# Quartered products of a four-layer graph network: three sums of the close formed in two GpSimd additions and one VectorE addition, and a new order of the products

## The chip, the cores and the metric

The kernel runs on one core of a Trainium2 chip. A core has five engines that run side by side, each taking its instructions in order: TensorE (PE in the profile; its weight loads are PEld) multiplies matrices and writes only to PSUM, an accumulator memory of eight banks; VectorE (DVE) and ScalarE (ACT) work element by element and read PSUM and SBUF, the on-chip working memory; GpSimd (POOL) works element by element in SBUF; SyncE (SP) issues DMA transfers. Semaphores order the engines among each other. The metric is the time on the device in microseconds (us), the median of several runs; lower is better.

## The reference

The input x has 128 graphs of 64 nodes with 512 features, fp32, and one 64x64 adjacency matrix. Four layers follow one another, each with h = relu(layernorm(x)) ahead of it and a residual sum after it:

```
layer 0:  q,k,v = h@Wq+bq, h@Wk+bk, h@Wv+bv  (8 heads of 64)
          x += softmax(q k^T / 8 + mask) v
layer 1:  the same, then @ Wo + bo
layer 2:  rel = adj^T * (q k^T);  rel /= norm(rel, axis=2);  x += rel v     (no heads)
layer 3:  as layer 1 without biases on q,k,v; o = attn @ w_proj + b_proj;  x += o + layernorm(o)*gamma + beta
```

## The kernel before

The rows of x (128 x 64 = 8192) are cut into 16 tiles of 512 rows. The loop over n = 0..63 goes through the layers, and within each layer through the 16 tiles. For a tile, `layer_norm` makes h, turns it with DMA transposes into hT (ScalarE copies hT out of the transposed halves hp), and `sums_x` forms the sums S on GpSimd that the fast matrix products need. Then the projections follow: q, k, v in layers 0, 1 and 3; in layer 2 g = h @ (Wq^T Wk), which has been folded once (`a2`), and v (`v2`). In layers 1 and 3 an output projection o of the tile before follows. Attention (`scores`, `attend`, `values`) or `relate` (layer 2) stands between.

Each projection is a 512x512x512 product, computed by Winograd's form of Strassen's scheme: seven products of 256-wide halves, numbered 1 to 7, in place of eight. On PE one such product is four fp32 matmuls of 128x128 weights and 256 columns, recorded as eight. `projection` runs through them in a written order. Products 1 and 2 add up in one PSUM bank, 6 and 7 in a second, 5 and 3 in a third; product 4 has its own. Between the two of a bank, its content is read out: after 1, `s1` is a copy on ScalarE; after 6, `u2` is a VectorE sum of the bank and s1; after 5, `z5` is a copy on ScalarE; after 7, `u3` is a VectorE sum again. Four quadrants of the output come from them:

- Y11: the bank of 1 and 2, a copy on ScalarE (with the bias in layer 1's q and k)
- Y12: the bank of 5 and 3, plus u2, on VectorE
- Y22: u3 + z5, on GpSimd
- Y21: product 4, plus u3

In layers 1, 2 and 3 (the names in LEVEL2) product 4 is quartered: the same scheme is used once more on 128-wide quarters, seven small products in place of eight. Its part "4a" holds the small products 1, 5, 6, 4, and "4b" the small products 2, 7, 3, added on top of 4a in the same bank. Each part is a group of 128-column matmuls, eight records and six. After 4a, ScalarE copies two quarters of the bank into a small tile q (q0 and z5), and VectorE forms u2 = quarter + q0. 4b may add onto these quarters only when they have been read. After 4b, VectorE forms u3 = quarter + q0, and `close_2` finishes: three GpSimd additions put the shared sums into the base (the big u3, or the output tile in layer 3's o), and two VectorE additions of the bank and the base write Y21. 159 projections are quartered: 16 tiles times q, k, v, o in layer 1, g, v in layer 2, q, k, v, o in layer 3, without the last o. The last tile's v has an order of its own, LAST_V.

The order in which all this is issued is not the order of the code. `Plan` records every step with its readers and writers, and `Plan.order` schedules them in a model of the five queues: of the steps of an engine that are ready it takes the one of lowest rank. The rank is the place in the recorded order, less RUSH = 100 places for a step that reads a PSUM bank (a tile named mm_), and ahead of all for the later steps of scores and values. So PE can take another product in between, or swap two, where the plan holds one as not ready. Pool.take and Pool.give hand the eight banks round, oldest first.

The orders are these tuples; ORDER serves layer 0, and FINER the quartered projections:

```
ORDER = (1, 6, 5, 2, 7, 3, 4)
FINER = (1, 6, 5, "4a", 2, 7, 3, "4b")
LAST_V = (1, 6, "4a", 5, 7, "4b", 2, 3)
```

The profile puts every instruction on one line, L221, since the plan issues them all there; tiles tell them apart. In the profile's names mm is a bank, u the tiles u2 and u3, s the tile s1 (and the attention scores), z the tile z5 (and others), q the small tile of the quartered product, xo the output tile of layer 1's o (it shares its buffers with the residual rows), kT also the output tile of layer 3's o.

Of the kernel before, what the change touches and what calls it, by code (L numbers as in the profile page):

```python
# [14 lines left out]
AF = mybir.ActivationFunctionType  # L15
# [3 lines left out]
P = 128  # L19
G = 64  # L20
D = 512
# [21 lines left out]
BLOCKS = {1: W11, 2: W21, 3: W22, 4: WT4, 5: WT1, 6: WT2, 7: WT3}  # L43
ORDER = (1, 6, 5, 2, 7, 3, 4)

FINER = (1, 6, 5, "4a", 2, 7, 3, "4b")
LAST_V = (1, 6, "4a", 5, 7, "4b", 2, 3)
ORDER0 = (1, 2, 5, 6, 3, 7, 4)

# [9 lines left out]
class Plan:  # L59
# [4 lines left out]
    def __init__(self, nc):  # L64
        self.nc = nc
        self.steps, self.products, self.lags, self.front = [], [], {}, set()
        self.wrote, self.readers, self.known = {}, {}, {}
        self.group = None
        for e in ("tensor", "vector", "scalar", "gpsimd", "sync"):
            setattr(self, e, Engine(self, e))  # L70

# [79 lines left out]
    def order(self):  # L151
        n = len(self.steps)
        wait = [0] * n
        users = [[] for _ in range(n)]
        for i, s in enumerate(self.steps):
            lags = {**self.lags.get(i, {}), **{d: 0.0 for d in s[2]}}
            wait[i] = len(lags)
            for d, lag in lags.items():
                users[d].append((i, lag))

        rank = [i - (n if i in self.front else 0) - RUSH * any(v.tensor.name.startswith("mm_") for c in s[1] for v in c[1][1:] if isinstance(v, bass.AP)) for i, s in enumerate(self.steps)]
        ready = [0.0] * n
        free = {e: 0.0 for e in ("tensor", "vector", "scalar", "gpsimd", "sync")}
        added = 0.0
        moved = 0.0
        port = 0.0
        soon = {e: [] for e in free}
        here = {e: [] for e in free}
        for i in range(n):
            if not wait[i]:  # L170
                heapq.heappush(soon[self.steps[i][0]], (0.0, rank[i], i))
        out = []
        while len(out) < n:
            best = None
            for e in free:
                while soon[e] and soon[e][0][0] <= free[e]:
                    heapq.heappush(here[e], heapq.heappop(soon[e])[1:])
                if here[e]:
                    at = free[e]
                elif soon[e]:  # L180
                    at = soon[e][0][0]
                else:
                    continue
                if best is None or at < best[0]:
                    best = (at, e)
            at, e = best
            if not here[e]:
                while soon[e] and soon[e][0][0] <= at:
                    heapq.heappush(here[e], heapq.heappop(soon[e])[1:])
            i = heapq.heappop(here[e])[1]  # L190
            eng, calls, _, busy, late = self.steps[i]
            moves = calls[0][0] == "dma_start"
            if e == "gpsimd":
                busy += max(0.0, port - at)
            if moves and e == "gpsimd":
                moved = max(moved, at) + 8000
                added = max(added + 6000, at + 8500)
                late = added - at - busy
            elif e == "sync":
                moved = max(moved, at + 1400) + late / (170 if calls[0][2].get("transpose") else 280)  # L200
                late = moved + 600 - at - busy
            elif e == "vector" and late == PORT:
                busy += max(0.0, free["gpsimd"] - at)
                port = at + busy
            free[e] = at + busy
            out.append((at, i))
            for u, lag in users[i]:
                same = self.steps[u][0] == e
                ready[u] = max(ready[u], at + busy - lag + (0.0 if same and not moves else late))
                wait[u] -= 1  # L210
                if not wait[u]:
                    heapq.heappush(soon[self.steps[u][0]], (ready[u], rank[u], u))
        self.start = {i: at for at, i in out}
        self.span = max(free.values())
        return [i for _, i in sorted(out)]
# [90 lines left out]
def gnn_stack_kernel(  # L306
# [293 lines left out]
    def quarter(t, prod, i, j):  # L600
        u, v = (j, i) if prod is prod_T else (i, j)
        return t[:, u, v * P : (v + 1) * P]
# [8 lines left out]
            a, b = (ws[i], x) if prod is prod_T else (x, ws[i])  # L611
            pe.matmul(out, a, b, start=i == 1, stop=True, skip_group_check=True)

    def close_2(prod, ps, q, base, dst, bias):

        u2, u3, z5 = q[:, 1], q[:, 2], q[:, 3]
        y12 = quarter(base, prod, 0, 1)
        gps.tensor_tensor(y12, y12, u2, ALU.add)
        y2 = base[:, :, P:] if prod is prod_T else base[:, 1, :].rearrange("p (v f) -> p v f", v=2)
        gps.tensor_tensor(y2, y2, u3.unsqueeze(1).to_broadcast([P, 2, P]), ALU.add)  # L620
        gps.tensor_tensor(dst[:, 1, P:], base[:, 1, P:], z5, ALU.add)
        for at in ((slice(None), 0, slice(None)), (slice(None), 1, slice(0, P))):
            if bias is None:
                dve.tensor_tensor(dst[at], ps[at], base[at], ALU.add)
            else:
                dve.scalar_tensor_tensor(dst[at], ps[at], bias[at[1]], base[at], ALU.add, ALU.add)

    def projection(prod, name, xop, nm, emit, order=None):
        w = W[name]
        order = order or (FINER if finer(name) else ORDER)  # L630

        banks = {}
        tmp = {}

        def bank(i):
            banks[i] = mm.take(f"{i}_{nm}")
            return banks[i]

        def tmp_tile(tag):
            tmp[tag] = p1.tile([P, D], F32, tag=tag, name=f"{tag}_{nm}")  # L640
            return tmp[tag]

        X = {1: 1, 2: 1, 6: 6, 7: 6, 5: 5, 3: 5, 4: 4, "4a": "4a", "4b": "4a"}
        for i in order:
            home = X[i]
            first = home == i
            ps = bank(home) if first else banks[home]
            plan.begin()
            if i in BLOCKS:
                prod(ps, w[:, BLOCKS[i]], xop()[i], first)  # L650
            else:
                pv = ps.rearrange("p (u v) -> p u v", u=2)
                prod_2(prod, pv, name, xop(), (1, 5, 6, 4) if i == "4a" else (2, 7, 3))
            plan.end()
            if i == 1:
                act.copy(tmp_tile("s1"), ps)
            elif i == 2:
                emit("Y11", ps)
            elif i == 6:
                dve.tensor_tensor(tmp_tile("u2"), ps, tmp["s1"], ALU.add)  # L660
                emit("u2", tmp["u2"])
            elif i == 5:
                emit("z5", ps, tmp_tile("z5"))
            elif i == 7:
                dve.tensor_tensor(tmp_tile("u3"), ps, tmp["s1"], ALU.add)
                emit("u3", tmp["u3"])
                emit("Y22", tmp["u3"], tmp["z5"])
            elif i == 4:
                emit("Y21", ps, tmp["u3"])
            elif i == 3:  # L670
                emit("Y12", ps, tmp["u2"])
            elif i == "4a":
                q = p1.tile([P, 4, P], F32, tag="q", name=f"q_{nm}")
                act.copy(q[:, 0], quarter(pv, prod, 0, 0))
                dst, base, bias = emit("close")
                if bias is None:
                    act.copy(q[:, 3], quarter(pv, prod, 0, 1))
                else:
                    act.activation(q[:, 3], quarter(pv, prod, 0, 1), AF.Identity, bias=bias[1])
                dve.tensor_tensor(q[:, 1], quarter(pv, prod, 1, 1), q[:, 0], ALU.add)  # L680
            elif i == "4b":
                dve.tensor_tensor(q[:, 2], quarter(pv, prod, 1, 1), q[:, 0], ALU.add)
                if base is None:
                    base = tmp["u3"].rearrange("p (u v) -> p u v", u=2)
                close_2(prod, pv, q, base, dst, bias)
            if i in (2, 7, 3, 4, "4b"):
                mm.give(f"{home}_{nm}")
            if i != order[-1]:
                yield
# [3 lines left out]
    def emit_plain(region, shared=gps):  # L693

        def emit(what, a=None, b=None):
            if what == "close":
                return region(1, 0), None, None
            if what in ("u2", "u3"):
                return
            if what == "z5":  # L700
# [12 lines left out]
    def emit_bias(region, bias):  # L713

        def emit(what, a=None, b=None):
            if what == "close":
                return region(1, 0), None, (bias[:, 0:1], bias[:, 1:2])
            if what in ("u2", "u3"):
                return
            if what == "z5":  # L720
# [240 lines left out]
    def emit_out3(n, o):  # L961
# [5 lines left out]

        def emit(what, a=None, b=None):
            if what == "close":
                return reg(1, 0), reg(1, 0), None  # L970
            v2 = lambda t: t.rearrange("p (u v) -> p u v", u=2)
            if what == "u2":
                gps.tensor_tensor(v2(a), v2(a), bc(1), ALU.add)
# [332 lines left out]
```

## Time and profile before

| | us |
|---|---|
| median of 3 runs | 2827.89 (2827.47 to 2830.86) |
| profiled execution | 2826.41 |
| its span, first to last instruction | 2824.6 |
| PE busy | 2804.5 (99%) |
| VectorE busy | 1796.5 (64%) |
| ScalarE busy | 1500.7 (53%) |
| GpSimd busy | 1974.4 (70%) |
| granted PE clock | 0.999 |

The busy time of an engine is the time in which it has at least one instruction at work. The chain of work that ended last is on PE for 90% of the span. A row such as "PE mm <- DVE u: 2.2, 1, 2.2" in the list of waits says that PE stood still for 2.2 us in all, once, and that the instruction which let it go was VectorE's that writes u. In rows by form, the numbers after the bar are the busy time in us and the mean of one in ns.

### The profile page before, as it was taken

How to read it: one execution, taken by the hardware profiler on the slowest of the kernel's cores; microseconds unless marked ns; L12 is line 12 of the kernel's file. 1: busy time of each engine (PE TensorE's matmuls, PEld its weight loads, DVE VectorE, ACT ScalarE, POOL GpSimd, SP SyncE). 2: the span in 40 equal slices, each digit the busy share in tenths (PEclk: the TensorE clock that was granted, in tenths of full speed). 3: DMA queues.
4: the chain of work that ended last, by engine and by line, in shares of the span. 5: the costliest groups of instructions: out<-in, count | busy, mean ns of one | idle time of the engine just before them, and what ended most of it. 6: DMA issues, size and time to landing. Idle time of an engine off the chain costs nothing.

```text
span 2824.6 us, 65745 instructions
## 1 busy us (share of the span) xinstructions
PE 2804.5 (99%) x26787; PEld 2482.6 (88%) x26787; DVE 1796.5 (64%) x3346; ACT 1500.7 (53%) x2111; POOL 1974.4 (70%) x2008
## 2 busy tenths in 40 slices
PE   9999999999999999999999999999999999999998
PEld 8888788888888888888888888888888888888887
DVE  6666566765656556556545565655568777677676
ACT  4566557556564654645644444443545546556452
POOL 6555565557867677677678755556788887887885
PEclk9999999999999999999999999999999999999999
DMA  6566567556555555646556766566644655554553
GB/s 157 137 153 149 125 157 149 122 136 157 113 106 109 105 102 105 111 85 109 117 109 122 174 150 161 143 157 154 131 91 91 117 97 91 117 102 91 109 90 64
DMA packets 634447, 343.55 MB, mean 122 GB/s; under 512 B 484257, under 2 KB 565409, under 8 KB 634145
## 3 DMA queue, kind: packets, MB, share of 16 engines
q1 hardware_dynamic: 600880, 273.30, 43.0%
q0 software_dynamic: 33264, 66.06, 14.5%
q8 instruction: 209, 3.42, 0.5%
q14 instruction: 94, 0.76, 0.1%
HBM read 120.10 MB, written 102.76 MB: 79 GB/s over the span
## 4 chain that ended last, share of the span: by engine, by line
PE 90%; POOL 3%; DMA 2%; DVE 2%; ACT 1%; issue 1%; SPq 1%; POOLq 0%; DVEq 0%; ACTq 0%
PE mm L221 90%; POOL S L221 1%; POOL w L221 1%; SPq L221 1%; DMA xin<-in_x_dram 1%; DMA hp<-z 1%; POOL s L221 0%; DVE st L221 0%; ACT s L221 0%; DMA xin<-x 0%; DMA x<-xo 0%; ACT z L221 0%; POOL u L221 0%; DVE u L221 0%; ACT hT L221 0%
## 5 line engine op out<-in xcount | busy, mean ns | idle before, releaser
L221 PE MATMUL mm<-S,w 128*128 128x256 f32 x3584 | 814.5, 380 | 2.2 <-DVE u L221 2.2
L221 PEld LDWEIGHTS mm<-S,w 128*128 128x128 f32 x3584 | 678.5, 190 | 95.3 <-DVE u L221 2.6
L221 PE MATMUL mm<-hT,w 128*128 128x256 f32 (+1 forms) x3040 | 609.0, 346 | 0.0
L221 PEld LDWEIGHTS mm<-hT,w 128*128 128x128 f32 x3040 | 506.8, 191 | 55.4 <-issue 0.5
L221 DVE TENSOR_TENSOR u<-mm,s 128x512 f32<-128x512 f32 x414 | 284.6, 687 | 366.3 <-PE mm L221 295.0
L221 PE MATMUL mm<-w,S 128*128 128x256 f32 x2048 | 470.6, 381 | 1.3 <-ACT z L221 1.2
L221 PEld LDWEIGHTS mm<-w,S 128*128 128x128 f32 x2048 | 385.2, 190 | 55.7 <-ACT z L221 1.6
L221 ACT COPY hT<-hp 128x1024 uint16<-128x1024 uint16 x252 | 333.4, 1352 | 140.0 <-DMA hp<-z 139.5
L221 PE MATMUL mm<-w,hT 128*128 128x256 f32 (+1 forms) x1696 | 349.0, 348 | 2.5 <-DVE s L221 2.5
L221 PEld LDWEIGHTS mm<-w,hT 128*128 128x128 f32 x1696 | 284.4, 191 | 35.0 <-DVE s L221 3.7
L221 POOL TENSOR_TENSOR qT<-u,z 128x512 f32<-128x512 f32 x64 | 86.3, 1348 | 308.7 <-DVE u L221 254.4
L221 ACT COPY s<-mm 128x512 f32<-128x512 f32 x211 | 123.0, 585 | 323.8 <-PE mm L221 242.0
L221 DVE COPY z<-xin 128x1024 uint16<-128x1024 uint16 x252 | 271.9, 1095 | 34.8 <-ACT xin L221 27.2
L221 ACT COPY s<-hp 128x1024 uint16<-128x1024 uint16 x188 | 243.6, 1350 | 8.0 <-DMA hp<-z 7.7
L221 ACT ACTIVATE xin<-xin,nb,rs 128x512 f32<-128x512 f32 x256 | 194.7, 813 | 68.7 <-DVE nb L221 68.6
L221 POOL TENSOR_TENSOR S<-hT 128x512 f32<-128x512 f32 x126 | 162.8, 1292 | 91.6 <-ACT hT L221 91.6
L221 ACT COPY z<-s 128x1024 uint16<-128x1024 uint16 x188 | 192.2, 1047 | 64.8 <-POOL s L221 64.7
L221 PE MATMUL mm<-w,SO 128*128 128x256 f32 x992 | 224.7, 379 | 0.5 <-issue 0.5
L221 POOL TENSOR_TENSOR s<-s,mx 128x1024 f32<-128x1024 f32 x96 | 181.2, 1905 | 58.3 <-DVE mx L221 55.5
L221 POOL TENSOR_TENSOR u<-u,q 128x128 f32<-128x128 f32 (+1 forms) x288 | 180.3, 633 | 54.9 <-DVE q L221 45.4
L221 ACT ACTIVATE s<-s 128x1024 f32<-128x1024 f32 (+1 forms) x112 | 108.0, 967 | 207.8 <-POOL s L221 113.2
L221 PEld LDWEIGHTS mm<-w,SO 128*128 128x128 f32 x992 | 188.0, 190 | 26.1 <-DVE mx L221 0.7
(130 smaller groups left out, 4157.3 us busy)
## 6 DMA issues: line engine op xcount, KB each, us to landing
xin<-x SPq DMA_DIRECT2D x128, 256.0 KB, 3.7
xin<-in_x_dram SPq DMA_DIRECT2D x64, 256.0 KB, 3.8
x<-row POOLq DMA_DIRECT2D x16, 1024.0 KB, 14.0
x<-xo POOLq DMA_DIRECT2D x16, 1024.0 KB, 9.8
xin<-out_dram SPq DMA_DIRECT2D x64, 256.0 KB, 3.6
out_dram<-row POOLq DMA_DIRECT2D x16, 1024.0 KB, 11.1
out_dram<-xo POOLq DMA_DIRECT2D x15, 1024.0 KB, 9.9
out_dram<-xo SPq DMA_DIRECT2D x36, 256.0 KB, 2.5
```

The lines of the kernel that those rows point to most:

```text
L221: getattr(getattr(self.nc, eng), op)(*a, **k)
```

## The change

FINER is reordered: after 4a comes product 7, then 4b, then 3, and product 2 last. VectorE gets one more addition after 4b: z5 += u3 (both 128 x 128 in SBUF). The slots of the tile q are chosen by `shared_2` so that u2 and u3 lie side by side in the order in which their target quarters lie in the base. `close_2` then has two GpSimd additions in place of three: one of 128 x 256 that adds both to the two middle quarters (`mid`), and one of 128 x 128 that writes the last quarter as base + z5. Both are put into `hot`, a set of steps that get the same RUSH in rank as steps that read a bank. The emit functions return `mid` as well. ORDER, LAST_V and layer 0 stay.

```diff
--- before.py
+++ after.py
@@ -43,7 +43,7 @@
 BLOCKS = {1: W11, 2: W21, 3: W22, 4: WT4, 5: WT1, 6: WT2, 7: WT3}
 ORDER = (1, 6, 5, 2, 7, 3, 4)
 
-FINER = (1, 6, 5, "4a", 2, 7, 3, "4b")
+FINER = (1, 6, 5, "4a", 7, "4b", 3, 2)
 LAST_V = (1, 6, "4a", 5, 7, "4b", 2, 3)
 ORDER0 = (1, 2, 5, 6, 3, 7, 4)
 
@@ -66,6 +66,7 @@
         self.steps, self.products, self.lags, self.front = [], [], {}, set()
         self.wrote, self.readers, self.known = {}, {}, {}
         self.group = None
+        self.hot = set()
         for e in ("tensor", "vector", "scalar", "gpsimd", "sync"):
             setattr(self, e, Engine(self, e))
 
@@ -158,7 +159,14 @@
             for d, lag in lags.items():
                 users[d].append((i, lag))
 
-        rank = [i - (n if i in self.front else 0) - RUSH * any(v.tensor.name.startswith("mm_") for c in s[1] for v in c[1][1:] if isinstance(v, bass.AP)) for i, s in enumerate(self.steps)]
+
+        rank = [
+            i - (n if i in self.front else 0)
+            - RUSH * (i in self.hot or any(
+                v.tensor.name.startswith("mm_") for c in s[1] for v in c[1][1:] if isinstance(v, bass.AP)
+            ))
+            for i, s in enumerate(self.steps)
+        ]
         ready = [0.0] * n
         free = {e: 0.0 for e in ("tensor", "vector", "scalar", "gpsimd", "sync")}
         added = 0.0
@@ -611,14 +619,17 @@
             a, b = (ws[i], x) if prod is prod_T else (x, ws[i])
             pe.matmul(out, a, b, start=i == 1, stop=True, skip_group_check=True)
 
-    def close_2(prod, ps, q, base, dst, bias):
-
-        u2, u3, z5 = q[:, 1], q[:, 2], q[:, 3]
-        y12 = quarter(base, prod, 0, 1)
-        gps.tensor_tensor(y12, y12, u2, ALU.add)
-        y2 = base[:, :, P:] if prod is prod_T else base[:, 1, :].rearrange("p (v f) -> p v f", v=2)
-        gps.tensor_tensor(y2, y2, u3.unsqueeze(1).to_broadcast([P, 2, P]), ALU.add)
-        gps.tensor_tensor(dst[:, 1, P:], base[:, 1, P:], z5, ALU.add)
+    def shared_2(prod, q):
+
+
+        i, j = (1, 2) if prod is prod_N else (2, 1)
+        return q[:, 0], q[:, i], q[:, j], q[:, 3]
+
+    def close_2(prod, ps, q, base, mid, dst, bias):
+
+        for a, b, c in ((mid, mid, q[:, 1:3]), (dst[:, 1, P:], base[:, 1, P:], q[:, 3])):
+            plan.hot.add(len(plan.steps))
+            gps.tensor_tensor(a, b, c, ALU.add)
         for at in ((slice(None), 0, slice(None)), (slice(None), 1, slice(0, P))):
             if bias is None:
                 dve.tensor_tensor(dst[at], ps[at], base[at], ALU.add)
@@ -629,8 +640,7 @@
         w = W[name]
         order = order or (FINER if finer(name) else ORDER)
 
-        banks = {}
-        tmp = {}
+        banks, tmp = {}, {}
 
         def bank(i):
             banks[i] = mm.take(f"{i}_{nm}")
@@ -671,18 +681,22 @@
                 emit("Y12", ps, tmp["u2"])
             elif i == "4a":
                 q = p1.tile([P, 4, P], F32, tag="q", name=f"q_{nm}")
-                act.copy(q[:, 0], quarter(pv, prod, 0, 0))
-                dst, base, bias = emit("close")
+                q0, u2, u3, z5 = shared_2(prod, q)
+                act.copy(q0, quarter(pv, prod, 0, 0))
+                dst, base, mid, bias = emit("close")
                 if bias is None:
-                    act.copy(q[:, 3], quarter(pv, prod, 0, 1))
+                    act.copy(z5, quarter(pv, prod, 0, 1))
                 else:
-                    act.activation(q[:, 3], quarter(pv, prod, 0, 1), AF.Identity, bias=bias[1])
-                dve.tensor_tensor(q[:, 1], quarter(pv, prod, 1, 1), q[:, 0], ALU.add)
+                    act.activation(z5, quarter(pv, prod, 0, 1), AF.Identity, bias=bias[1])
+                dve.tensor_tensor(u2, quarter(pv, prod, 1, 1), q0, ALU.add)
             elif i == "4b":
-                dve.tensor_tensor(q[:, 2], quarter(pv, prod, 1, 1), q[:, 0], ALU.add)
+                dve.tensor_tensor(u3, quarter(pv, prod, 1, 1), q0, ALU.add)
+                dve.tensor_tensor(z5, z5, u3, ALU.add)
                 if base is None:
-                    base = tmp["u3"].rearrange("p (u v) -> p u v", u=2)
-                close_2(prod, pv, q, base, dst, bias)
+                    t = tmp["u3"]
+                    base = t.rearrange("p (u v) -> p u v", u=2)
+                    mid = t[:, P : 3 * P].rearrange("p (u v) -> p u v", u=2)
+                close_2(prod, pv, q, base, mid, dst, bias)
             if i in (2, 7, 3, 4, "4b"):
                 mm.give(f"{home}_{nm}")
             if i != order[-1]:
@@ -694,7 +708,7 @@
 
         def emit(what, a=None, b=None):
             if what == "close":
-                return region(1, 0), None, None
+                return region(1, 0), None, None, None
             if what in ("u2", "u3"):
                 return
             if what == "z5":
@@ -714,7 +728,7 @@
 
         def emit(what, a=None, b=None):
             if what == "close":
-                return region(1, 0), None, (bias[:, 0:1], bias[:, 1:2])
+                return region(1, 0), None, None, (bias[:, 0:1], bias[:, 1:2])
             if what in ("u2", "u3"):
                 return
             if what == "z5":
@@ -967,7 +981,8 @@
 
         def emit(what, a=None, b=None):
             if what == "close":
-                return reg(1, 0), reg(1, 0), None
+                mid = o.rearrange("p t d -> p (t d)")[:, 2 * D + P :][:, : 2 * (D - P)]
+                return reg(1, 0), reg(1, 0), mid.rearrange("p (u v) -> p u v", u=2)[:, :, :P], None
             v2 = lambda t: t.rearrange("p (u v) -> p u v", u=2)
             if what == "u2":
                 gps.tensor_tensor(v2(a), v2(a), bc(1), ALU.add)
```

## The prediction

> **What bounds the kernel now.** I read the page's busy line first.
>
> ```profile
> PE 2804.5 (99%) x26787; PEld 2482.6 (88%) x26787; DVE 1796.5 (64%) x3346; ACT 1500.7 (53%) x2111; POOL 1974.4 (70%) x2008
> ```
>
> TensorE (PE) is busy for all but 20 us of the 2824.6 us span. The list of waits, for PE alone, says what is left to gain.
>
> ```profile
> PE mm L221 <- ACT xin L221: 2.5, 1, 2.5
> PE mm L221 <- DVE s L221: 2.5, 2, 1.7
> PE mm L221 <- DVE u L221: 2.2, 1, 2.2
> PE mm L221 <- POOL ident masks.py:199: 1.4, 1, 1.4
> PE mm L221 <- ACT z L221: 1.2, 1, 1.2
> PE mm L221 <- DVE kT L221: 1.2, 3, 0.6
> ...
> ```
>
> Columns: total us, times, longest. With three small rows (0.5, 0.4, 0.2) PE waits 12.1 us in all. 3.9 of these (xin, ident) belong to the start of the program. Busy time by stretches, cut at the layer boundaries, shows where the other 8.2 are not.
>
> ```profile
> 650.00:1477.00 827.00, 827.00 (x8130) 738.54 (x8129) 479.41 (x905) 454.27 (x670) 606.50 (x647) 1.00 0.57 109
> 1597.00:1964.00 367.00, 366.98 (x3056) 325.16 (x3054) 218.59 (x498) 163.27 (x246) 207.58 (x247) 1.00 0.61 154
> 1969.00:2736.00 767.00, 767.00 (x7400) 684.71 (x7399) 554.85 (x998) 411.82 (x584) 629.29 (x653) 1.00 0.54 102
> ```
>
> After the length, the columns are PE, its weight loads, DVE, ACT and POOL. Inside layers 1, 2 and 3, where the changed code runs, PE has no gap. What the change can win lies in a few microseconds at the boundaries; what it can lose is anything that makes PE wait.
>
> One quartered product in layer 2, from the timeline (start, duration):
>
> ```profile
> 1778.95 0.39 PE L221 MATMUL mm<-hT,w 128*128 128x128 f32 x2
> 1779.17 0.61 PE L221 MATMUL mm<-s,w 128*128 128x128 f32 x4
> ...
> 1779.62 2.12 PE L221 MATMUL mm<-hT,w 128*128 128x128 f32 x10
> 1781.01 1.34 ACT L221 COPY hT<-hp 128x1024 uint16<-128x1024 uint16 x1 [1.21 <-DMA hp<-z]
> 1781.57 3.62 PE L221 MATMUL mm<-S,w 128*128 128x256 f32 x16
> 1782.21 0.43 ACT L221 COPY q<-mm 128x128 f32<-128x128 f32 x2
> ...
> 1782.67 0.29 DVE L221 TENSOR_TENSOR q<-mm,q 128x128 f32<-128x128 f32 x1 [3.50 <-ACT q L221]
> ...
> 1785.03 0.38 PE L221 MATMUL mm<-hT,w 128*128 128x128 f32 x2
> ```
>
> The first part ("4a") is eight 128-column records at 0.11 us: two, four, and the first two of the x10; it ends at 1779.84. ScalarE must copy two quarters out of the bank and VectorE must form one sum before the second part ("4b") may add to them. ScalarE sits behind a copy of hT that waits for its transpose, so the sum ends at 1782.96, 3.12 us after 4a. Nothing stops: 4b starts at 1785.03, because three whole products at 1.73 us (two take 1781.57 to 1785.03) stand between.
>
> [...] nb<-mv,rs, four elements and both inputs in SBUF, takes 477 ns in the mean and 0.16 us where GpSimd is idle.
>
> **The change, part by part.** 159 projections are quartered (q<-mm,q counts 318, two each).
>
> *Removed on GpSimd:* one 128x128 addition per projection. The row u<-u,q of that shape has a mean of 524 ns: 159 x 0.524 = 83 us of 1974. The 256-wide addition (743 ns) and the last 128-wide one stay. PE waits for no such row, so its direct worth is nothing inside the layers; at the boundaries it may be 0 to 3 us.
>
> *Added on VectorE:* z5 += u3, 128x128, both inputs in SBUF. No row has this shape and place. From below it is the sum q<-mm,q at 284 ns; [...] I take 0.29 + 0.3 [...] the excess that nb<-mv,rs shows: 159 x 0.6 = 95 us. Idle time of VectorE, 36% of the span, hides it. Queued behind it are the two sums that close the product and the next evacuation. Without the cover each would be 0.6 us late: 95 us at worst, 0 taken.
>
> *Moved: earlier rank for the two GpSimd additions.* They pass the sums S and SO and the accumulating DMAs that GpSimd issues; those start up to 0.74 + 0.52 us later. The sums feed the next tile, tens of us away: nothing. No DMA is added, on SP's queue or GpSimd's.
>
> *Moved: product 2 to the end.* Its copy Y11 on ScalarE is the last writer of the region. For k, the scores wait for it: one copy of 0.59 or two of 0.42 us, against the DVE and POOL chain of before. In the projections o of layer 1 this copy waited for the DMA on its output tile and blocked ScalarE; moving it later helps there. I take -1.5 us for this and the relieved boundaries together, 0 to -5 as its bounds.
>
> *Moved: 4b ahead of 3 and 2.* This decides. The build's order of instructions shows at least three products between 4a and 4b in 145 of 159 cases before; after, product 7 alone in 78, two products in 76. (A planner orders the work, and puts 3 ahead when it expects a late evacuation.) With product 7 alone, 4b comes 1.73 us after 4a; the copy must be done by then, the sum 0.22 us later, for the second quarter product. In the pictured case the sum would be 3.12 - 1.95 = 1.17 us late. I paired all 159 in the trace of before this way, each against the number of products that the new order gives it: layer 1, 6 late cases, 7.5 us; layer 2, 15 cases, 17.7 us; layer 3, 1 case, 0.6 us. Together 25.8 us if ScalarE and VectorE queued as before and every delay were paid in full.
>
> They don't. A wait of PE shifts all later work, so a backlog is paid once and not again for each product. And the new order puts one of the two hT copies behind the q copies in most layer 2 tiles: 1.34 us less in the pictured case, which leaves 1.78 us against 1.95, no wait, unless the other hT copy is late too. I take one third, 8.6 us, with 0 and 25.8 as the ends. What is late next is the sum of product 7 and 4b on VectorE; these release banks for products that start 3 us or more later.
>
> Sum: 8.6 - 1.5 + 0 + 0 = +7.1 us on the profiled execution's 2826.4 (span 2824.6 plus 1.8 around it). The median of the runs, 2827.9, is 1.5 above that, so 2835.0.
>
> **The rivals.**
>
> *No measurable change.* The planner knows of the queues and puts product 3 ahead of 4b where they are full; then 4b waits seldom. For it: 81 of 159 cases have other work there, and PE stands still nowhere inside the layers today, under the same planner. Against it: in layer 2 the evacuation came a median 2.96 us after 4a, and 19 of 32 cases have only 1.73. It gives 0 to +5 us, about 2830.
>
> *Faster, by the boundaries.* GpSimd with 83 us less work finishes the sums of new weights and the last evacuations of a layer sooner, and Y11 no longer blocks ScalarE. The waits for DVE s, DVE u, ACT z, DVE kT and DVE v sum to 7.5 us; if all went, 2820.4. It decides when more than 5.7 us net go. Against it: the largest, 2.5 and 2.2, end with VectorE work behind DMAs (xin, and x<-xo), which GpSimd's load does not govern.
>
> *VectorE becomes late.* If the added sum waits [...] and one in ten of these delays reaches PE through the next evacuation, 16 us more: 2851. For it: GpSimd is 70% busy. Against it: the idle third of VectorE.
>
> **How the numbers follow.** About 0.2% (5.7 us) is what a measurement can tell from no change here, so same means 2822.2 to 2833.5. My forecast, PE waiting ahead of 4b, 0.53; late VectorE, 0.07; no measurable change, 0.32; faster, 0.08. The first two end slower, but for a low tail of the forecast's: 0.57 slower, 0.35 same, 0.08 faster. The range runs from 2825 (no waits, 3 us won) to 2850 (nearly all 25.8 paid, or the late VectorE).
>
> **What would show it.** PE's waits gain rows for ACT q and DVE q, most in layer 2, few in layer 3; PE's busy records stay at 26787 or so and near 2804 us. GpSimd falls to about 1890 us, VectorE rises by 50 to 100. The new z5 sum has a mean of 0.3 to 0.7 us. Wrong would be: no PE wait on q; or waits before the scores on ACT kT, when Y11 is the late one; or a span shorter by over 5.7 us, which needs the boundary waits gone.

## The result, and the profile after

The changed kernel takes 2845.94 us (median of 4 runs, 2842.40 to 2848.27), the kernel before 2828.11 us beside it: ratio 1.006, 95% interval 1.0043 to 1.0078. It is slower by 17.8 us. A second measurement, on another chip, gave 2847.29 us against 2828.32, ratio 1.0071 (1.0058 to 1.0084). The profiled execution took 2842.4 us with a span of 2840.6, against 2826.41 and 2824.6 before: +16.0 us. This difference is what the traces have to explain.

The busy line of the page after:

```profile
PE 2809.0 (99%) x26787; PEld 2479.6 (87%) x26787; DVE 1873.7 (66%) x3505; ACT 1492.1 (53%) x2111; POOL 1884.6 (66%) x1849
```

PE has the same 26787 records and 4.5 us more busy time. GpSimd lost 90 us, VectorE gained 77. So PE is still the bound, and 16.0 - 4.5 = 11.5 us are idle time of PE. Its waits, largest first (total, times, longest, in us):

```profile
PE mm L229 <- DVE q L229: 15.0, 2, 10.8
PE mm L229 <- issue: 2.7, 1, 2.7
PE mm L229 <- ACT xin L229: 1.6, 2, 1.4
PE mm L229 <- POOL ident masks.py:199: 1.4, 1, 1.4
PE mm L229 <- DVE u L229: 1.2, 1, 1.2
...
```

With five small rows (0.6, 0.4, 0.3, 0.2, 0.2) they sum to 23.6 us, where they summed to 12.1 before: +11.5. The row DVE q is new and worth 15.0; all others fell from 12.1 to 8.6. And it has two waits, not twenty. The 2.7 us on issue are new as well: one wait at 764 us, in the midst of a group of score products, which nothing that the trace shows ended. In every run below that keeps this plan the longest wait on issue is 2.1 to 3.3 us, so it is not what tells them apart. The busy time by the three stretches inside the layers says where they are not (columns as before: length, PE, PEld, DVE, ACT, POOL, clock):

```profile
650.00:1477.00 827.00, 813.50 (x8049) 723.78 (x8048) 502.24 (x955) 451.30 (x662) 560.86 (x577) 0.99 0.56 108
1597.00:1964.00 367.00, 366.41 (x3045) 322.64 (x3044) 235.06 (x535) 162.11 (x248) 191.43 (x221) 1.00 0.62 152
1969.00:2736.00 767.00, 766.44 (x7365) 682.25 (x7364) 580.24 (x1060) 406.45 (x582) 597.93 (x591) 1.00 0.54 105
```

In these stretches of layers 2 and 3 PE has 1.2 us of gaps in 1134. The large wait, 10.8 us, stands at 714 us, in v of tile 16, the first tile of layer 1; the other, 4.2 us, at 1539 us, in v of tile 32, the first of layer 2. In both, PE has done 4a and may not start 4b until q has been read. The timeline of after around the large one (start, duration, then in brackets the idle time of that engine and what ended it):

```profile
704.61 1.48 POOL L229 DMA_DIRECT2D x<-row  x1
706.05 1.79 POOL L229 DMA_DIRECT2D x<-row  x1
...
706.36 3.17 SPq L229 DMA_TRANSPOSE hp<-z  x1
...
710.06 1.16 PE L229 MATMUL mm<-w,hT 128*128 128x128 f32 x8
711.06 3.62 PE L229 MATMUL mm<-w,S 128*128 128x256 f32 x16
723.45 1.33 ACT L229 COPY hT<-hp 128x1024 uint16<-128x1024 uint16 x1 [13.11 <-DMA hp<-z]
724.65 0.42 ACT L229 COPY q<-mm 128x128 f32<-128x128 f32 x2
725.10 0.29 DVE L229 TENSOR_TENSOR q<-mm,q 128x128 f32<-128x128 f32 x1 [7.37 <-ACT q L229]
725.44 0.80 PE L229 MATMUL mm<-w,hT 128*128 128x128 f32 x2 [10.77 <-DVE q L229]
```

Read it upwards. PE's 4b (725.44) waits for VectorE's q sum, that for ScalarE's copies of q, and these stand on ScalarE behind an hT copy that waited 13.11 us for its transpose. 4a was done by 711.2; only two products (711.06 to 714.68) covered what followed. The chain of work that ended last puts the whole of it on one transfer:

```profile
706.36 17.06 DMA hp<-z
```

This is the fourth and last transpose of the next tile. From issue to landing the transposes take 3.3 us in the median in both kernels (444 of them, not all with a recorded landing); the longest is 8.2 us before and this one after. What stands ahead of it are the two DMAs x<-row: GpSimd adds the bias row onto x of tiles 16 and 17 in DRAM, 1 MB each. Such a DMA, which adds onto what stands at its target, is called accumulating here. In the kernel before, the same instructions stand in the other order:

```profile
707.56 1.23 SPq L221 DMA_TRANSPOSE hp<-z  x1
708.35 2.81 POOL L221 DMA_DIRECT2D x<-row  x2
711.88 1.35 ACT L221 COPY hT<-hp 128x1024 uint16<-128x1024 uint16 x1 [2.38 <-DMA hp<-z]
```

The last transpose had been issued 0.79 us ahead of the pair, and its copy came 4.3 us after issue. In after the pair comes 3.74 us earlier, the transpose only 1.20 us earlier, and so 1.75 us behind the first of the pair. The wait at 1539 us has the same form: GpSimd issues the accumulating x<-xo of tile 30 at 1529.96 (before: 1540.94), a transpose issued at 1530.39 follows it, its hT copy waits 8.16 us, and PE stands still for 4.19 us ahead of 4b. The chain has it too:

```profile
1530.39 10.22 DMA hp<-z
```

A late landing costs time only where PE's next work hangs on it: in the same profile a transpose issued at 837.45 lands 10.0 us later, and PE has no wait there.

A second loss hides in PE's busy time. The same columns for the stretches at the two waits; the clock is the third figure from the end:

```profile
718.02:728.26 10.24, 2.82 (x10) 2.55 (x11) 3.14 (x6) 1.61 (x3) 3.32 (x3) 0.50 0.59 87
...
1544.05:1547.46 3.41, 3.41 (x11) 2.78 (x10) 0.93 (x2) 0.43 (x1) 2.40 (x3) 0.50 0.70 219
```

In these stretches the granted clock is half, and PE works 2.82 and 3.41 us of them. Eight records of 256 columns, which took 1.89 us at 1537.33, took 3.46 at 1544.31, so half of that work is taken as lost, an estimate: 1.4 + 1.7 = 3.1 us. The first stretch is three times as long as the second, 10.24 and 3.41 us. The first begins 3.34 us after PE stopped. The second begins at 1544.05, 0.63 us after PE went back to work at 1543.42, so all of it falls on work: by the estimate the half clock cost 1.7 us at the shorter wait, 1.4 at the longer one. What starts and what ends such a stretch was not shown.

The profile before has such a stretch as well, at the start of the program, which the profile after lacks:

```profile
8.26:11.67 3.41, 3.41 (x17) 3.41 (x18) 0.40 (x3) 2.12 (x3) 2.87 (x5) 0.50 1.01 250
```

By the same estimate it is worth 1.7 us. The sum: 15.0 (new waits) - 3.5 (other waits) + 3.1 (half clock at them) - 1.7 (half clock at the start) + 3.1 (other busy time, not explained) = 16.0 us.

### The profile page after: what moved, and what is told of

Read it like the earlier page. It is cut to its first block, busy times and chain, and to the rows that moved or that the text cites. A ratio compares the mean times of both kernels' runs of the same rounds, so it can differ in the third digit from the quotient of the medians.

```text
span 2840.6 us, 65632 instructions
## 1 busy us (share of the span) xinstructions
PE 2809.0 (99%) x26787; PEld 2479.6 (87%) x26787; DVE 1873.7 (66%) x3505; ACT 1492.1 (53%) x2111; POOL 1884.6 (66%) x1849
## 4 chain that ended last, share of the span: by engine, by line
PE 94%; DMA 2%; DVE 2%; issue 1%; SPq 1%; ACT 1%; POOL 1%; POOLq 0%; DVEq 0%; ACTq 0%
PE mm L229 94%; DMA hp<-z 1%; SPq L229 1%; DVE xo L229 0%; DMA xin<-in_x_dram 0%; POOL rn L229 0%; DMA xin<-x 0%; DVE st L229 0%; ACT z L229 0%; ACT s L229 0%; DVE z L229 0%; DVE u L229 0%; DVE kT L229 0%; ACT xin L229 0%; ACT hT L229 0%
## 5 line engine op out<-in xcount | busy, mean ns | idle before, releaser
L229 PEld LDWEIGHTS mm<-S,w 128*128 128x128 f32 x3584 | 670.2, 190 | 88.3 <-DVE xo L229 1.0
L229 PE MATMUL mm<-hT,w 128*128 128x256 f32 (+1 forms) x3040 | 618.4, 346 | 0.2 <-ACT s L229 0.2
L229 PEld LDWEIGHTS mm<-hT,w 128*128 128x128 f32 x3040 | 517.6, 190 | 60.8 <-ACT s L229 0.8
L229 PE MATMUL mm<-w,S 128*128 128x256 f32 x2048 | 480.9, 383 | 1.2 <-DVE u L229 1.2
L229 PEld LDWEIGHTS mm<-w,S 128*128 128x128 f32 x2048 | 379.4, 191 | 53.2 <-DVE u L229 1.6
L229 PE MATMUL mm<-w,hT 128*128 128x256 f32 (+1 forms) x1696 | 350.9, 347 | 15.5 <-DVE q L229 15.0
L229 PEld LDWEIGHTS mm<-w,hT 128*128 128x128 f32 x1696 | 293.1, 191 | 52.7 <-DVE q L229 18.1
L229 DVE COPY z<-xin 128x1024 uint16<-128x1024 uint16 x252 | 227.1, 924 | 32.2 <-ACT xin L229 24.7
L229 DVE TENSOR_TENSOR q<-mm,q 128x128 f32<-128x128 f32 x318 | 91.4, 287 | 183.1 <-ACT q L229 169.6
L229 DVE BATCH_NORM_STATS2 st<-xin 128x6 f32<-128x512 f32 x256 | 172.5, 674 | 50.8 <-DMA xin<-x 29.7
```

The costliest lines, as they stand in the source:

```text
L229: getattr(getattr(self.nc, eng), op)(*a, **k)
```

## The experiments

The theory, called T in the expectations: the loss is a collision. The plan now issues accumulating DMAs of 1 MB ahead of transposes that the next products need, and what stands behind a late transpose on ScalarE and VectorE carries the delay to PE (723.45 to 725.44 in the timeline above). The rival: the loss belongs to the new order of products (O in the expectations) or to the new close with its VectorE sum (V), wherever the DMAs stand. All ratios are against the kernel before on the same chip. Chips differ, and only ratios can be compared between them. The kernel before took 2822.84 us beside the runs with the pair or three DMAs moved, with the pair put ahead in the old kernel, and with the order alone; 2825.99 beside those with one of the pair moved and with the new close alone; 2828.32 beside the others.

**Only the DMAs moved.** The plan's whole order of after is kept, and one or more of GpSimd's accumulating DMAs are put in again at a place that is later by so many ns of the plan, ahead of whatever depends on them. The helper:

```diff
+    def shifted(self, order, which, by):
+        adds = [i for i in order if self.steps[i][0] == "gpsimd" and self.steps[i][1][0][0] == "dma_start"]
+        for w in which:
+            i = adds[w]
+            to = self.start[i] + by
+            order.remove(i)
+            at = sum(self.start[j] <= to for j in order)
+            ...
+                at = min([at] + [k for k, j in enumerate(order) if i in self.steps[j][2]])
+            order.insert(at, i)
+        return order
...
-        for i in self.order():
+        for i in self.shifted(self.order(), (1, 0), 8000):
```

First the pair x<-row (numbers 0 and 1) by 8 us:

> The changed kernel with its whole planned order kept on every engine, but the two accumulating DMAs of the bias row (x<-row, 1 MB each, at 704.6 and 706.1 us in the profile after) are issued by GpSimd about 8 us later, when all four transposes of the next tile have landed. Theory T (a transpose caught behind these DMAs blocks ScalarE, and with it the second part of product 4): the 10.8 us wait of PE at 714 us and the half-speed clock after it (1.4 us) go; profiled execution 2830 and median 2834, within 2 us. Rival O (the order of the products makes the wait, the DMAs only happen to be there): PE still waits 8 us or more for q near 714; 2842 to 2846. Rival V (the added VectorE sum and the regrouped close cost small waits everywhere): no more than 2 us changes.

2834.49 us, ratio 1.0035 (1.0027 to 1.0044). The pair is now issued at 715.50 and 717.75, the last hT copy comes at 711.50 after waiting 0.84 us, and the 10.8 us wait is gone. The wait at the start of layer 2 stays, 5.4 us here; the mean granted clock is 0.998, against 0.997 with the whole change. The time is the one that T named, but the kernel before is faster on this chip, so more of the loss remains than T had it. One of the 14 executions took 2823.25 us, the others 2832.25 to 2837.04; it has no trace, and it may be one in which the second wait did not come. Then also x<-xo of tile 30 (number 30), by the same 8 us:

```diff
-        for i in self.order():
+        for i in self.shifted(self.order(), (30, 1, 0), 8000):
```

> As the run before, and the accumulating DMA x<-xo that GpSimd issues at 1530 us in the profile after is issued about 8 us later too, after the transposes of its tile. T: also the 4.2 us wait at 1539 and 1.7 us of half-speed clock go; profiled execution about 2825, median 2827 to 2830, the time of the kernel before within 2 us. O: still 2842 to 2846. V: no more than 2 us below the changed kernel.

2825.07 us, ratio 1.0005 (0.9998 to 1.0013): no measurable difference from the kernel before. The first waits of PE:

```profile
PE mm L243 <- issue: 2.9, 2, 2.5
PE mm L243 <- ACT xin L243: 1.5, 1, 1.5
...
```

No wait on q is left. Three instructions of 65632 were moved; order, close, rank and the added VectorE sum are all there. This shows that, with this plan, the whole loss hangs on where these three DMAs are issued, and the rival falls for the change as a whole. One of the pair alone, the second, gives the dose (it came to stand at 723.19, far behind the transposes):

```diff
-        for i in self.order():
+        for i in self.shifted(self.order(), (1,), 8000):
```

> The changed kernel with its planned order kept, and only the second of the two x<-row DMAs issued 8 us later; the first one stays where it is, ahead of the last transpose. A dose: 1 MB in place of 2 MB ahead of the transpose. T: the transpose waits about half as long (landing 8 to 11 us in place of 15 to 17), so the wait of PE near 714 shrinks from 10 us to between 1 and 5; ratio 1.003 to 1.005 with the second wait still there. If the wait stays at 9 us or more, the size of the DMAs ahead is not what sets it; if it goes altogether, the second DMA alone did.

2839.85 us, ratio 1.0051 (1.0037 to 1.0065). With 1 MB ahead of it the hT copy of the transpose starts 11.5 us after its issue (718.00 and 706.47), not 17.1, and PE's first wait is 5.0 us, not 10.8: about half. The second wait, 4 us, stays in both. The landing and the ratio lie just above what T expected, and the interval of the ratio overlaps that of the whole change: the dose is seen in the trace, not in the time.

**The collision put into the kernel before.** The old plan is kept, and the pair is issued about 5 us earlier:

```diff
-        for i in self.order():
+        for i in self.shifted(self.order(), (0, 1), -5000):
```

> The kernel before (old order of products, old close) with its planned order kept, but the two x<-row DMAs are issued about 5 us earlier, ahead of the last transpose of the next tile. T: the transpose lands some 17 us after its issue in place of 3.3, ScalarE's copy of hT and the q copies behind it come 12 us late, and the old order covers 5.2 us of that with three products where the new one covers 3.5 with two: PE waits 7 to 10 us for q near 715, half-speed clock after it, 2835 to 2840. O: the old order hides it; under 2831. V: 2828.

2837.59 us, ratio 1.0047 (1.0035 to 1.0059). The pair is issued at 704.59 and 706.03, and two transposes are caught. The one issued at 705.62 lands after 15.7 us, for the hT copy at 721.32; the last one, at 710.16, after 15.1 us, for the copy at 725.31:

```profile
705.62 1.33 SPq L235 DMA_TRANSPOSE hp<-z  x1
710.16 10.76 SPq L235 DMA_TRANSPOSE hp<-z  x1
721.32 1.33 ACT L235 COPY hT<-hp 128x1024 uint16<-128x1024 uint16 x1 [13.26 <-DMA hp<-z]
722.58 0.69 DVE L235 BATCH_NORM_STATS2 st<-xin 128x6 f32<-128x512 f32 x1 [11.70 <-DMA xin<-x]
723.19 0.67 DVE L235 TENSOR_TENSOR u<-mm,s 128x512 f32<-128x512 f32 x1
723.92 5.83 PE L235 MATMUL mm<-w,S 128*128 128x256 f32 x16 [7.28 <-DVE u L235]
725.31 1.34 ACT L235 COPY hT<-hp 128x1024 uint16<-128x1024 uint16 x1 [2.66 <-DMA hp<-z]
```

PE's largest wait is 7.3 us, and it is on u, not on q as T had it. The sum u stands on VectorE behind a statistic of the next layernorm, which waited 11.70 us for its load xin<-x. That load of 256 KB was issued at 707.04, behind the pair too, and landed after 15.5 us (median of such loads before: 3.7). So the collision is no property of the new code: it costs the old kernel too, and it catches loads as well as transposes. As the chain is another one, 7.3 and 10.8 us do not tell how much the order of the products covers.

**What brought the DMAs forward.** The changed kernel without the earlier rank:

```diff
-            plan.hot.add(len(plan.steps))
```

> The changed kernel without the earlier rank of the two GpSimd additions (nothing is put into hot). The planned place of the x<-row DMAs against the transposes at the start of layer 1 is the same as in the changed kernel, so T expects the 10 us wait at 714 us again and a ratio of 1.004 to 1.007; if the earlier rank of the GpSimd work is what brings the DMAs forward, the wait goes and the ratio is under 1.002. The last accumulating DMAs of layer 1 stand otherwise in this plan, so the second wait, of 4 us, may go or stay.

2849.32 us, ratio 1.0076 (1.0062 to 1.0090), a little above what T expected. The pair stands at 704.85 and 706.30, the hT copy waits 13.76 us, PE 10.2. The rank is not what moves the DMAs. It does something else:

```profile
PE mm L229 <- DVE q L229: 15.6, 15, 10.2
...
```

Fifteen waits instead of two, thirteen of them of 0.2 to 0.8 us in layer 3. The kernel before with the new FINER alone:

```diff
-FINER = (1, 6, 5, "4a", 2, 7, 3, "4b")
+FINER = (1, 6, 5, "4a", 7, "4b", 3, 2)
```

> The kernel before with the new FINER order alone; close and shared sums as before. In this build the planner issues the two x<-row DMAs where the kernel before has them, after the last transpose. T: no wait over 3 us at the start of layer 1; 2826 to 2833, unless a transpose is caught elsewhere. O: most of the loss is there, 2840 or more. V: 2828 to 2831, since the close is the old one.

2850.17 us, ratio 1.0088 (1.0074 to 1.0101): slower than the whole change, where T had expected little. The pair is at 706.33, the last transpose 0.58 us after it, and its copy waits 3.46 us: half a collision. Most of the loss is of another kind:

```profile
PE mm L221 <- DVE q L221: 5.1, 7, 1.6
PE mm L221 <- DVE u L221: 3.6, 3, 2.4
PE mm L221 <- ACT z L221: 3.3, 4, 1.0
...
```

These are many small waits in layers 1 to 3, on q among others: the mechanism that the prediction had in mind, with the old close. But PE's waits sum to 19.6 us, only 7.5 more than in the profile before; its busy time is 10.5 us longer at a clock of 0.999, and that is not explained. The other half, the changed kernel with the old FINER:

```diff
-FINER = (1, 6, 5, "4a", 7, "4b", 3, 2)
+FINER = (1, 6, 5, "4a", 2, 7, 3, "4b")
```

> The changed kernel with the old FINER order (product 2 after 4a, 4b last): the new close, the added VectorE sum and the earlier rank of the two GpSimd additions alone. In this build the two x<-row DMAs stand 1.4 us behind the last transpose of the plan instead of ahead of it by a fraction; whether it is caught is open. T: the loss is what caught transposes cost, 7 to 10 us if one is caught with three products of cover, else none: ratio to the kernel before 1.000 or 1.003. V (the added VectorE sum costs small waits everywhere): waits of PE for q or u in each tile, ratio 1.004 or more without any wait over 3 us.

2861.71 us, ratio 1.0123 (1.0107 to 1.0138), the slowest of all; T expected 1.003 at most.

```profile
PE mm L229 <- ACT z L229: 19.4, 14, 4.0
PE mm L229 <- DVE q L229: 8.6, 1, 8.6
...
```

Again one collision (the pair at 710.20, the last transpose at 711.36, its copy waits 11.98 us). The 19.4 us are new: ScalarE's copy z5 waits for a GpSimd instruction that reads the one buffer of z5 (at 880.05 for 3.35 us), and GpSimd is late there. The same without the earlier rank, which is the new close alone on the kernel before, in `close_2` and its callers:

```diff
-        gps.tensor_tensor(y12, y12, u2, ALU.add)
-        gps.tensor_tensor(y2, y2, u3.unsqueeze(1).to_broadcast([P, 2, P]), ALU.add)
-        gps.tensor_tensor(dst[:, 1, P:], base[:, 1, P:], z5, ALU.add)
+        for a, b, c in ((mid, mid, q[:, 1:3]), (dst[:, 1, P:], base[:, 1, P:], q[:, 3])):
+            gps.tensor_tensor(a, b, c, ALU.add)
...
+                dve.tensor_tensor(z5, z5, u3, ALU.add)
```

> The kernel before with the new close alone: two GpSimd additions and one VectorE sum in place of three GpSimd additions; old order of products, old ranks. It tells what the 159 added VectorE sums cost by themselves. V: small waits of PE for DVE q or u through layers 1 to 3, ratio 1.004 or more. T: none of these; a wait of 7 to 9 us near 715 only if the last transpose is caught behind the x<-row DMAs, ratio 1.000 to 1.001 without and 1.003 to 1.005 with it.

2854.44 us, ratio 1.0099 (1.0085 to 1.0114). The pair is at 704.76 and 706.88; two hT copies wait 8.96 and 7.94 us, PE 3.5 and 6.8, and a dozen waits of 0.5 to 2.5 us are spread over all layers. T expected 1.005 at most; the ratio and the spread of the waits are nearer to what V expected. So the order alone brings the pair forward by 2.0 us and the close alone by 3.6. Why the plan does so in each case is not visible in a trace; GpSimd has less queued ahead of them in the new close, which is argued and not tested. T explains the loss of the whole change; of these partial versions, which have plans of their own, it explains only the waits behind caught transposes. Their small waits were not followed up.

**A version faster than both?** The three DMAs still later, the pair by 12.5 us, behind all sums of the tile:

```diff
-        for i in self.order():
+        for i in self.shifted(self.shifted(self.order(), (30,), 8000), (1, 0), 12500):
```

> As the run with three DMAs later, but the x<-row DMAs go behind the sums S of the next tile on GpSimd (12.5 us later than in the changed kernel), so that these sums are not held up by the issue of 1.5 to 1.8 us each. T: no wait over 2 us at 714 and 1539; the small wait of 1.3 us for z5 near 726 stays or shrinks; ratio 0.999 to 1.001. If it is below 0.999, this version beats the kernel before.

2828.24 us, ratio 1.0001 (0.9993 to 1.0008). With these two collisions gone the change is worth nothing that can be measured, and no version here beats the kernel before. Late transposes stay in both versions: the longest landing is 10.5 us with three DMAs moved and 12.2 here, and PE's longest wait on issue 2.5 and 2.1 us. In the profile after, such a transpose, issued at 755.83, lands after 8.0 us; it stands behind the next x<-row, issued at 754.79, and PE's wait on issue, 2.7 us, ends at 764.17. Whether the two belong together, and whether moving this DMA too would pay, was not tested. The changed kernel measured again beside it:

> The changed kernel itself, on the chip of these runs, as their measure: the ratio of 1.006 again (1.004 to 1.008), with one wait of PE for q of about 10 us near 714 and one of about 4 us near 1539.

2847.29 us, as given above. The two waits are there again, 9.5 and 1.6 us, the pair at 704.33, the transpose at 706.46, its copy waiting 10.54 us. The lengths of the two waits differ between the two profiles of this kernel, 10.8 and 4.2 us against 9.5 and 1.6, which may be why its runs spread over 6 to 10 us.

## Why the prediction was right in sign and wrong in place

*Slower, 2825 to 2850, likeliest 2835.* The sign and the range held; 2845.94 is 10.9 us above the likeliest. That the range held is in good part luck: the time was lost in two places that the sum did not have, by an event that it put at nothing.

*GpSimd -83 us, VectorE +95 us.* They came to -90 and +77. The added sum has its own row:

```profile
L229 DVE TENSOR_TENSOR q<-q 128x128 f32<-128x128 f32 x159 | 143.7, 904 | 3.8
```

Its mean of 904 ns is above the 0.3 to 0.7 us forecast: of the excess over 0.29 us, 0.6, the estimate of 0.3 was half. The excess goes with GpSimd's work. In the profile after, the 19 of these sums that started with no GpSimd instruction at work took 0.29 us in the mean, the other 140 took 0.99, and each of the 140 ended after that instruction. One of them:

```profile
751.81 1.27 POOL L229 TENSOR_TENSOR kT<-u,z 128x512 f32<-128x512 f32 x1 [6.68 <-DVE u L229]
751.94 1.29 DVE L229 TENSOR_TENSOR q<-q 128x128 f32<-128x128 f32 x1
```

That VectorE rose by 77 us and not by 143.7 is because other rows fell; the largest is z<-xin, 271.9 us before and 227.1 after. That the total came near the forecast is luck to that extent. VectorE's idle third hid the new row all the same: the version with three DMAs moved has it at 919 ns and loses nothing. The rival "VectorE becomes late" falls with that, for the change as a whole.

*Boundaries -1.5 us.* Without the start of the program and the new wait on issue, the waits other than q fell from 8.2 to 2.9 us: the sign was right, the size a little past the bound of 5. Which part of the change did it was not tested.

*4b ahead of 3 and 2: +8.6 us.* The kind was right: every large wait is PE ahead of 4b, for VectorE's q, because ScalarE's q copy stands behind an hT copy that waits for its transpose. Place and size were wrong. No row of ACT q came. The pairing gave 15 late cases in layer 2; the trace has none after its first tile. The pairing took the queues of before as they were, while the plan rearranged them, and the order alone shows what happens without the new close and rank: small waits do come. And the pairing could hold no landing later than the 8.2 us that the trace of before contains. The term came to 15.0 us in two waits.

*Moved: "those start up to 0.74 + 0.52 us later", nothing.* This is the step that failed. The accumulating DMAs were considered for lateness only, and as to their own users, who have tens of us. They came earlier, 3.7 us for the pair and 11 for the third, and so ahead of SP's transposes. It is the whole loss: moving the three to a later place takes the ratio to 1.0005. The two queues share the DMA engines: between 704 and 724 us the accumulating queue took 63.4% of the 16 engines' time and the queue with the transposes 44.9%, together over 100% (packets of the two overlap in time). In the kernel before it was 59.0 and 38.2% in the same stretch, so the load is much the same and the order is what differs. The price itself, 17.1 us in place of 3.3, is what the traces show.

*The half clock* was no step of the sum; at the two waits it added 3.1 us, by the estimate above.

*No measurable change* was the rival with 0.32. It is what the change is worth with the three DMAs out of the way, so its argument, that the plan avoids waits for q, holds for all but the two places.

## What to carry to other kernels

When an edit shifts an order, list the large transfers that change places with small ones which an engine waits for with other work behind them, in both directions: earlier is not free. In this kernel a 1 MB accumulating DMA belongs behind the transposes that the next products need (17.1 us to landing after the two, 3.3 in the median). To test such a cause, keep the whole order and move only the suspects; undoing parts of the edit lets a planner rearrange everything, and the parts do not add up (1.0088 and 1.0123 for the halves, 1.006 for the whole).

## What the runs showed of the hardware

A DMA transpose, 3.3 us to landing in the median, took 10.2 us behind one accumulating DMA of 1 MB in the profile after (the second wait) and about 11.5 us with one of the pair moved. With both of the pair about it, it took 17.1 us, 15.5 in the second profile of the changed kernel, and 15.7 and 15.1 in the old kernel with the pair put ahead. There a load of 256 KB took 15.5 us. SP's issue of such a transpose, mostly 1.23 us, grew to 3.17 and 5.61 us in the profile after, and to 10.76 in the old kernel with the pair put ahead. From 3.34 us into a wait of 10.8 us TensorE had half the clock for 10.24 us, 2.8 us of it work; from 0.63 us after one of 4.2 us it had half the clock for 3.41 us, all of it work.
